# A perceiver kernel on one core: the second layers of the tiles ahead of the last are placed in fewer, denser pieces

## The chip, the cores and the metric

The kernel runs on one NeuronCore of a Trainium2 chip. The metric is the device time of one execution in microseconds (us). Before the change the median of three runs is 2055.67 us (2054.99 to 2056.97).

## What is computed

The input is 32 sequences of 64 rows and 256 columns, and for each sequence a context of 1601 rows of 256 columns. Two layers follow each other, each residual:

```python
x = x + L0_xattn(layernorm(x), ctx)    # a linear layer of x and of the mean of the context
x = x + L0_attn(layernorm(x))          # 16 heads, 64 keys
x = x + L0_ffn(layernorm(x))           # shared and routed experts
x = x + L1_xattn(layernorm(x), ctx)    # 16 heads over all 1601 context rows
x = x + L1_attn(layernorm(x))          # causal convolution, minimal GRU, gated feed-forward
x = x + L1_ffn(layernorm(x))           # two quantised linear layers with a gelu between
```

The last two lines are what the kernel calls the second layer of a tile. In L1_attn each part is normalised by its root mean square, then: a depthwise convolution of 4 taps and a 256x256 linear layer; gates per head and a first-order recurrence over 64 rows; silu(n w_gate) * (n w_value) w_out with 682 inner columns. L1_ffn rounds its activations to 8 bits by the row's largest absolute value, multiplies by ternary weights (256x1024), applies gelu, rounds again and multiplies by ternary weights (1024x256).

## The kernel before, in words

The 2048 rows are 16 tiles of 128 rows (two sequences each), taken in the order of `order`; `pos` counts them from 0 to 15. Nearly all time goes to L1_xattn. Its context is cut into pieces: 13 for each tile (`NU`), so the main loop runs over 208 pieces, `for g in range(NU * NT)`. One pass is called a slot here. Slots 195 to 207 belong to the last tile.

The order of the instructions on TensorE, VectorE, ScalarE and GpSimd is written out by hand (`tc.manual_schedule`), and each engine works its instructions in that order. TensorE's order in a slot g is:

1. `column_scores(g)`: scores `s` (L845, L851); ScalarE then makes two exponentials `pt` (L857) out of them, into a pair of PSUM buffers `sc` that scores and row scores share.
2. `maxima_rows`, in every third slot, and `values(g + 4)`: `vps` (L236), copied to `vau` by VectorE (L787).
3. place 0: steps of the other layers.
4. `row_scores(g + 5)`: `r` (L803), whose maxima `mx` VectorE takes (L810); in every third slot five short instructions follow (`maxima`).
5. place 0.5, then `weighted(g)`: `o` (L875), which needs both `pt` and collects the output.
6. `keys(g + 6)`: `kps` (L248), copied to `kt` by ScalarE (L770).
7. place 1: steps of the other layers. Here `in_columns` is set, and `mmq` splits a matmul into four of 32 columns, as the keys are.

The last slots have less: `values` end with slot 203, row scores with slot 202 and keys with slot 201.

All other layers are generators, cut into steps by `yield`. An object of the class `Steps` (L1245) runs a generator's steps over a stretch of slots: `planned(gen, t0, t1, n, place)` (L1337) spreads n steps evenly from t0 to t1 (in sixteenths of a tile). With place 3, at most one step runs at a place, and the value that the last `yield` gave says at which one: `ACT` at place 0, `COL` at place 0.5, anything else at place 1. What is left after the last slot runs in turns, one step of each generator at a time, in the loop `while plan` at the end of the function, together with the second layer of the last tile; this stretch is called the drain here.

The second layer of a tile (`recurrent`, then `bit_ffn`) has 30 steps. Those with TensorE work are marked PE:

```
 1 moments e (L192-L197)           11 PE tp_f, nT            21 PE ff (second half), th, m
 2 xn_e, yb                        12 PE hg, tanh gg zz, rr  22 m
 3 square, rn_e                    13 zz, gg, gg             23 PE ffo, x5, moments h
 4 xs_e                            14 gg, cc, scan           24 xn_h, am_h, qt, q_h
 5 PE tp_e, ypad                   15 PE gru, y2, xy         25 PE tpq_h, qT_h
 6 convolution, first half         16 square, rn_g           26 PE h1, gelu (L1124)
 7 convolution, second half        17 xs_g                   27 am_i, qs_i, qd_i
 8 PE pw, y1                       18 PE tp_g, nT2           28 L1070, L1071, q_i (L1074)
 9 square, rn_f                    19 PE ff (first half), th, m   29 PE tpq_i, qT_i
10 xs_f                            20 m                      30 PE h2, x6, store
```

Their pace is set in one line of the plan, L1348 (33 steps over 29.5 sixteenths, some 24 slots):

```python
planned(second_layer(pos - 1), 16 * pos + 1.5, 16 * pos + 31, 33, 3)
```

Counted out, this gives for the last three tiles that run in the loop: tile 12 (by position) from slot 171 to slot 191; tile 13 from slot 184 to slot 204; tile 14 from slot 197 on, with steps 1 to 15 in the loop (8 in slot 202, 11 in slot 204, 12 in 205, 15 in 207) and steps 16 to 30 in the drain, in turns with the 30 steps of tile 15.

Of the kernel before, what the change touches and what calls it, by code (L numbers as in the profile page):

```python
# [15 lines left out]
P = 128  # L16
# [28 lines left out]
def perceiver_kernel(ctx: ExitStack, tc: tile.TileContext, a: dict, out: bass.AP):  # L45
# [16 lines left out]
    ACT = "ACT"  # L62

    COL = "COL"

    def sc_tile(name):
        return ps_sc.tile([P, 2, 512], F32, tag="sc", name=name)
# [137 lines left out]
    def rms_scaled(x, name):  # L205

        xs = work_tile([P, D], "xs", f"xs_{name}")
        ss = small.tile([P, 1], F32, tag="ss", name=f"ss_{name}", bufs=4)
        nc.scalar.activation(xs, x, AF.Square, accum_out=ss)
        rn = small.tile([P, 1], F32, tag="rn", name=f"rn_{name}", bufs=4)  # L210
        nc.gpsimd.tensor_scalar(rn, ss, 1e-24, None, ALU.max)
        nc.gpsimd.tensor_tensor(rn, rn, mhalf, ALU.pow)
        yield
        nc.vector.tensor_scalar(xs, x, rn, None, ALU.mult)
        return xs

# [37 lines left out]
    def silu_mul(m, u, v, th):  # L254

        nc.scalar.activation(th, u, AF.Tanh, scale=0.5)
        nc.vector.tensor_scalar(m, u, 0.5, None, ALU.mult)
        nc.vector.tensor_tensor(m, m, v, ALU.mult)
        yield
        nc.vector.scalar_tensor_tensor(m, th, 1.0, m, ALU.add, ALU.mult)  # L260


# [689 lines left out]
    def recurrent(ti, x):  # L952
        def tile_(shape, tag, name):
            return work_tile(shape, tag, f"{name}_{ti}")

        m = moments(x, f"e{ti}")
        yield
        y = normalised(tile_([P, D], "xnb", "xn_e"), m)
        yb = plus_row(tile_([P, D], "xbb", "yb"), y, R_PWB)
        yield ACT  # L960
        xs = yield from rms_scaled(y, f"e{ti}")
        yield ACT
        t = transposed_ps(xs, f"e{ti}")
        cT = tile_([P, 2, 2, S], "xs", "cT")
        for c in range(2):
            nc.scalar.activation(ypad[:, c, :, 3:], t[:, c, :].rearrange("p (b s) -> p b s", b=2), AF.Copy,
                                 scale=gains[:, c, 0:1])
        yield
        for c in range(2):
            nc.vector.tensor_scalar(cT[:, c], ypad[:, c, :, 3:], chv[:, c, DW + 3:DW + 4], chv[:, c, DWB:DWB + 1],  # L970
                                    ALU.mult, ALU.add)
            for j in range(3):
                nc.vector.scalar_tensor_tensor(cT[:, c], ypad[:, c, :, j:j + S], chv[:, c, DW + j:DW + j + 1],
                                               cT[:, c], ALU.mult, ALU.add)
            yield
        o = mm_tile([P, D], f"pw_{ti}")
        mmq2(o, lambda c: cT[:, c].rearrange("p b s -> p (b s)"), lambda c: w_pw[:, c, :])
        y = tile_([P, D], "xnewb", "y1")
        nc.vector.tensor_tensor(y, o, yb, ALU.add)  # L979
        yield ACT  # L980
        xs = yield from rms_scaled(y, f"f{ti}")
        yield ACT

        t = transposed_ps(xs, f"f{ti}")
        nT = tile_([P, 2, P], "xTb", "nT")
        for c in range(2):
            nc.scalar.activation(nT[:, c, :], t[:, c, :], AF.Copy, scale=gains[:, c, 1:2])
        yield ACT

        def gt(name):  # L990
            return tile_([P, 2, 2, P], "g2k", name)

        gg, zz, rr = gt("gg"), gt("zz"), gt("rr")

        nc.gpsimd.memset(rr[DI:, :, :, :], 0.0)

        hg = [mm_tile([DI, 2, 2, P], f"hg_{ti}_{h}") for h in range(2)]
        for part in range(2):  # L1000
            for c in range(2):
                for h in range(2):
                    r = slice(64 * h, 64 * h + 64)
                    nc.tensor.matmul(hg[h][:, part, c, :], lhsT=w_hg[r, c, part * DI:(part + 1) * DI],  # L1004
                                     rhs=nT[r, c, :], start=True, stop=True)
        for h in range(2):
            nc.scalar.activation(gg[:DI, h], hg[h][:, 0], AF.Tanh, scale=0.5)
            nc.scalar.activation(zz[:DI, h], hg[h][:, 1], AF.Tanh, scale=0.5)
            nc.vector.tensor_scalar(rr[:DI, h], hg[h][:, 0], 0.0, 0.5, ALU.max, ALU.add)
        yield  # L1010
        hT = rr
        gg, zz, rr = (t[:DI] for t in (gg, zz, rr))
        nc.gpsimd.tensor_scalar(zz, zz, 0.5, 0.5, ALU.mult, ALU.add)
        nc.vector.tensor_scalar(gg, gg, 0.0, 0.5, ALU.min, ALU.mult)
        nc.vector.tensor_tensor(gg, gg, rr, ALU.add)
        yield
# [12 lines left out]
        nc.vector.tensor_tensor(y2, o, y, ALU.add)  # L1029
        xy = tile_([P, D], "xbb", "xy")  # L1030
        nc.gpsimd.tensor_tensor(xy, x, y2, ALU.add)
        yield ACT
# [7 lines left out]
        yield ACT  # L1040
        m = tile_([P, NF, P], "w4k", "fm")
        for f0 in range(0, NF, 3):
            uv = [mm_tile([P, 3, P], f"ff_{ti}_{f0}_{j}") for j in range(2)]
            for o, w in zip(uv, (w_fg, w_fv)):
                for f in range(3):
                    mm2(o[:, f, :], lambda c: w[:, c, (f0 + f) * P:(f0 + f + 1) * P], lambda c: nT[:, c, :])
            th = tile_([P, 3, P], "g2k", f"fth{f0}")
            yield from silu_mul(m[:, f0:f0 + 3, :], uv[0], uv[1], th)
            yield ACT if f0 == 0 else None
        o = mm_tile([P, D], f"ffo_{ti}")  # L1050
        for f in range(NF):
            mmq(o, m[:, f, :], w_fo[:, f, :], f == 0, f == NF - 1)
        x = tile_([P, D], "xnewb", "x5")
        nc.vector.tensor_tensor(x, o, xy, ALU.add)
        return x


    def quantised(v, n, tmp, sw, name):
# [7 lines left out]
        d = small.tile([P, 1], F32, tag="qd", name=f"qd_{name}", bufs=4)  # L1066
        nc.vector.tensor_tensor(d, am, sw, ALU.mult)
        if n == HID:
            yield
# [42 lines left out]

    def bit_ffn(ti, x):
        m = moments(x, f"h{ti}")
        yield
# [3 lines left out]
        yield ACT  # L1119
        h = work_tile([P, HID], "w4k", f"h_{ti}")  # L1120
        for j in range(2):
            h_ps = mm_tile([P, 512], f"h1_{ti}_{j}")
            mm2(h_ps, lambda c: qT[:, c, :], lambda c: w_b1[:, c, 512 * j:512 * j + 512])
            nc.scalar.activation(h[:, 512 * j:512 * j + 512], h_ps, AF.Gelu, scale=d)  # L1124
        yield
# [119 lines left out]
    class Steps:  # L1245
# [15 lines left out]

        def run(self, t, place):
            at = place if self.place == 2 and place != 0.5 else self.place
            if self.place == 3:
                if {ACT: 0, COL: 0.5}.get(self.kind, 1) != place:
                    return
                at = place
            if at == place:
                now = t + (0.5 * place if self.place >= 2 else 0)
                while self.gen is not None and self.done * (self.t1 - self.t0) <= (now - self.t0) * self.n:  # L1270
                    self.step()
                    if self.place == 3:
                        break

        def all(self):
            while self.gen is not None:
# [65 lines left out]
    for pos in range(1, NT):  # L1342
# [2 lines left out]
            planned(first_layer(pos), t0, t0 + 27 - 4 * (pos == 3), 28, 3)  # L1345
        if pos < NT - 1:
            planned(queried(pos), 16 * (pos - 1) + (1 if pos > 1 else 5), 16 * (pos - 1) + 8.5, 6, 0)
        planned(second_layer(pos - 1), 16 * pos + 1.5, 16 * pos + 31, 33, 3)  # L1348
    for group, t0, t1 in ((range(4, 6), 5.5, 15), (range(6, 9), 16, 42), (range(9, 13), 45, 84), (range(13, 16), 88, 140)):
        planned(sums_of(group), t0, t1, 12 * len(group) + 2, 0)  # L1350
    for c, t0 in ((1, 72), (2, 128), (3, 184)):
# [132 lines left out]
```

## Time and profile before

| what | value |
|---|---|
| median of three runs | 2055.67 us |
| profiled execution, own time | 2057.83 us |
| its span | 2056.1 us |
| TensorE (PE) busy | 1959.6 us, 95% |
| VectorE (DVE) busy | 1300.7 us, 63% |
| ScalarE (ACT) busy | 903.2 us, 44% |
| GpSimd (POOL) busy | 325.5 us, 16% |
| slots 203 to 207 | 1954.33 to 1983.14 us from the span's start |
| drain | 1983.14 to 2056.10 us |

The profiled execution is 2.16 us over the median of the other runs. A row of the timeline gives the start, the summed duration, the engine, the line, the operation, output<-input with shapes, the number of instructions, and in brackets the idle time before it with what ended it. Matmuls of fp32 count as two instructions each. Durations of one matmul overlap with those of its neighbours, so what a group of matmuls costs is best read from start to start.

### The profile page before, as it was taken

How to read it: one execution, taken by the hardware profiler on the slowest of the kernel's cores; microseconds unless marked ns; L12 is line 12 of the kernel's file. 1: busy time of each engine (PE TensorE's matmuls, PEld its weight loads, DVE VectorE, ACT ScalarE, POOL GpSimd, SP SyncE). 2: the span in 40 equal slices, each digit the busy share in tenths (PEclk: the TensorE clock that was granted, in tenths of full speed). 3: DMA queues.
4: the chain of work that ended last, by engine and by line, in shares of the span. 5: the costliest groups of instructions: out<-in, count | busy, mean ns of one | idle time of the engine just before them, and what ended most of it. 6: DMA issues, size and time to landing. Idle time of an engine off the chain costs nothing.

```text
span 2056.1 us, 79668 instructions
## 1 busy us (share of the span) xinstructions
PE 1959.6 (95%) x36755; PEld 1368.4 (67%) x36771; DVE 1300.7 (63%) x2618; ACT 903.2 (44%) x1402; POOL 325.5 (16%) x543
## 2 busy tenths in 40 slices
PE   5889999999999999999999999999999999999974
PEld 3556676667676766666766676767666666666663
DVE  4556766666657766666667666666667666565544
ACT  4345455454546444444544434343443434334431
POOL 2121111111112111111111121211110111000011
PEclk9899999999999999999999999999999999999986
DMA  9224323221222212112120101111011111101000
GB/s 310 105 87 171 128 85 111 77 88 44 94 89 88 95 44 72 46 58 76 61 77 20 58 22 37 50 40 45 26 59 32 61 44 37 57 3 48 2 12 5
DMA packets 54806, 136.90 MB, mean 67 GB/s; under 512 B 13318, under 2 KB 35016, under 8 KB 54472
## 3 DMA queue, kind: packets, MB, share of 16 engines
q1 hardware_dynamic: 53912, 130.99, 18.6%
q8 instruction: 288, 4.72, 0.9%
q10 hardware_dynamic: 560, 0.81, 0.1%
q14 instruction: 46, 0.38, 0.1%
HBM read 125.53 MB, written 6.25 MB: 64 GB/s over the span
## 4 chain that ended last, share of the span: by engine, by line
PE 86%; DVE 8%; ACT 2%; issue 2%; POOL 1%; DMA 0%; SPq 0%; DVEq 0%; POOLq 0%; ACTq 0%
PE vps L236 17%; PE kps L248 15%; PE r L803 11%; PE o L875 9%; PE s L851 9%; PE ff L236 4%; PE s L845 3%; DVE mx L810 3%; PE ffo L248 2%; PE q L236 1%; ACT pt L857 1%; PE wo L248 1%; PE hg L1004 1%; PE k L236 1%; PE sv L236 1%
## 5 line engine op out<-in xcount | busy, mean ns | idle before, releaser
L857 ACT ACTIVATE pt<-s 128x1024 f32<-128x1024 f32 (+1 forms) x416 | 403.1, 1021 | 267.6 <-PE s L851 267.5
L810 DVE TENSOR_REDUCE mx<-r 128x2 f32<-128x1024 f32 x384 | 451.9, 1219 | 98.3 <-PE r L803 97.9
L236 PE MATMUL vps<-w_L_xattn_WvT,ctxT 128*128 128x128 f32 x3072 | 391.6, 281 | 2.3 <-DVE y L979 1.8
L770 ACT ACTIVATE kt<-kps,chv 128x512 f32<-128x512 f32 x192 | 132.0, 687 | 586.1 <-PE kps L248 568.6
L236 PEld LDWEIGHTS vps<-w_L_xattn_WvT,ctxT 128*128 128x128 f32 x3072 | 357.9, 191 | 22.2 <-issue 3.7
L248 PE MATMUL kps<-ctxT,w_L_xattn_WkT 128*32 128x512 f32 x2992 | 356.1, 593 | 0.0
L787 DVE COPY vau<-vps 128x512 f32<-128x512 f32 (+1 forms) x208 | 143.6, 691 | 313.9 <-PE vps L236 312.5
L875 PEld LDWEIGHTS o<-pt,vau 128*32 128x32 f32 (+1 forms) x13312 | 198.8, 110 | 132.2 <-issue 118.5
L875 PE MATMUL o<-pt,vau 128*32 128x64 f32 (+1 forms) x13312 | 231.1, 221 | 5.2 <-ACT pt L857 5.1
L803 PE MATMUL r<-kt,qbd 32*128 32x512 f32 x1536 | 229.2, 647 | 2.8 <-DVE mx L810 2.0
L851 PE MATMUL s<-qbd,kt 32*128 32x128 f32 x6144 | 209.6, 272 | 0.0
L851 PEld LDWEIGHTS s<-qbd,kt 32*128 32x128 f32 x6144 | 207.2, 188 | 3.1
L248 PEld LDWEIGHTS kps<-ctxT,w_L_xattn_WkT 128*32 128x32 f32 x2992 | 83.5, 110 | 112.7 <-issue 112.7
L803 PEld LDWEIGHTS r<-kt,qbd 32*128 32x128 f32 x1536 | 66.3, 184 | 40.6 <-issue 19.8
L845 PEld LDWEIGHTS <-onesb 3*128 3x128 bf16 x768 | 21.3, 91 | 104.0 <-issue 102.1
L845 PE MATMUL s<-neg,onesb 3*128 3x512 bf16 x768 | 82.8, 386 | 5.8 <-DVE mx L810 5.0
L294 ACT ACTIVATE part<-part 128x1601 f32<-128x1601 f32 x48 | 74.1, 1544 | 0.0
L236 PE MATMUL ff<-nT,w_fg 128*128 128x128 f32 x384 | 51.0, 285 | 1.0 <-ACT nT L1039 1.0
L370 POOL TENSOR_TENSOR kbd<-kT,mask 128x512 f32<-128x512 f32 x32 | 32.6, 1041 | 114.8 <-ACT kT L363 114.8
L236 PEld LDWEIGHTS ff<-nT,w_fg 128*128 128x128 f32 x384 | 47.9, 201 | 1.8 <-ACT nT L1039 1.8
L236 PE MATMUL ff<-nT,w_fv 128*128 128x128 f32 x384 | 48.5, 276 | 0.0
L417 POOL TENSOR_TENSOR s<-s,mx 128x1024 f32<-128x1024 f32 x15 | 28.5, 1903 | 115.2 <-DVE mx L401 115.2
(384 smaller groups left out, 2397.8 us busy)
## 6 DMA issues: line engine op xcount, KB each, us to landing
ctxT<-ctxT SPq DMA_DIRECT2D x31, 1601.0 KB
part<-ctxT SPq DMA_DIRECT2D x60, 800.5 KB
od<-osb SPq DMA_DIRECT2D x15, 256.0 KB
rest<-ctxT SPq DMA_DIRECT2D x32, 65.0 KB
x<-x SPq DMA_DIRECT2D x16, 128.0 KB
out<-x SPq DMA_DIRECT2D x16, 128.0 KB
w<-w SPq DMA_DIRECT2D x16, 128.0 KB
rs<-od SPq DMA_DIRECT2D x30, 64.0 KB
```

Of the source, the lines that this page charges most:

```text
L236: nc.tensor.matmul(o, lhsT=lhsT(c), rhs=rhs(c), start=(c == 0), stop=(c == 1))
L248: nc.tensor.matmul(o[r], lhsT=lhsT[:, r], rhs=rhs, start=start, stop=stop)
L294: nc.scalar.activation(parts[j], parts[j], AF.Copy, accum_out=csum[:, c, 2 * i + b:2 * i + b + 1])
L370: nc.gpsimd.tensor_tensor(kbd[oc], kT[:, oc, :].rearrange("p (b k) -> p b k", b=2).unsqueeze(2).to_broadcast([P, 2, 4, S]), mask4.unsqueez ...
L770: nc.scalar.activation(kt, o, AF.Identity, bias=chv[:, hf.oc, BK2:BK2 + 1])
L787: nc.vector.tensor_copy(v[:kr, :, 0:VW - 16].rearrange("p k (h d) -> p k h d", d=17)[:, :, :, 0:16], o[:kr].rearrange("p k (h d) -> p k h ...
L803: nc.tensor.matmul(o, lhsT=qbd[r, q % 2, q // 2].rearrange("p h q -> p (h q)"), rhs=w.kt[r, q, :] if h is None else halves[h].kt[k][r, :], ...
L810: nc.vector.tensor_reduce(w.mx[:, 2 * m:2 * m + 2, h % 4, k], ps[m], AX.X, ALU.max)
L845: nc.tensor.matmul(o, lhsT=onesb[r, :], rhs=halves[h].neg[r, :].unsqueeze(1).to_broadcast([3, 4, P]), start=True, stop=False)
L851: nc.tensor.matmul(ps[i // 2][:kr, i % 2, j * P:(j + 1) * P], lhsT=w.kt[r, j, :] if h is None else halves[h].kt[k][r, j * P:(j + 1) * P], ...
L857: nc.scalar.activation(pt[:kr].rearrange("p i k c -> p i (k c)"), ps[m][:kr], AF.Exp)
L875: nc.tensor.matmul(w.o[32 * c:32 * c + 32, q, m, :], lhsT=v[:kr, j, 17 * hd:17 * hd + 32], rhs=pts[m][:kr, c // 2, j, c % 2 * S:c % 2 * S ...
```

## The change

Three things are changed.

First, the second layers' `yield`s say more: `OFF` and `OFF_ACT` mean that the next step has no TensorE work, `ANY` that it may run at place 0 or at place 1 (the two halves of ff, and h1; for these `mm2` becomes `mmq2`, so that at place 1 they are split into columns). Under place 3 the new values mean what the old ones did.

Second, there is a place 4 (`paced`). At a place that is due it runs either one step with TensorE work (`ACT` at place 0, `None` at place 1, `ANY` at both), and behind it at place 1 also the steps without TensorE work that are due; or, if the next step has no TensorE work, all such steps that are due, up to the next one that has.

Third, the plan's line sets: tile 12 ends two sixteenths earlier under place 3, tile 13 runs 33 steps over 18.5 sixteenths under place 4, and tile 14 runs 38 over 13.5, also under place 4.

```diff
+        def paced(self, t, place):
+            due = (t + 0.5 * place - self.t0) * self.n / (self.t1 - self.t0)
+            made = False
+            while self.gen is not None and place != 0.5 and self.done <= due:
+                off = self.kind in (OFF, OFF_ACT) or self.done == 0
+                if made and (place == 0 or not off):
+                    break
+                if not off:
+                    if made is not False or self.kind != ANY and (0 if self.kind == ACT else 1) != place:
+                        break
+                self.step()
+                made = made or not off or None
...
-        planned(second_layer(pos - 1), 16 * pos + 1.5, 16 * pos + 31, 33, 3)
+        t1, n, place = {NT - 3: (29, 33, 3), NT - 2: (20, 33, 4), NT - 1: (15, 38, 4)}.get(pos, (31, 33, 3))
+        planned(second_layer(pos - 1), 16 * pos + 1.5, 16 * pos + t1, n, place)
```

Counted out by hand from this code, the steps stand so (slot.place; the numbers are the steps of the list above):

```
tile 12 before: ... 184.0 19  184.1 20  185.0 21  185.1 22  186.1 23  187.1 24  188.0 25  189.0 26  189.1 27  190.1 28  191.0 29  191.1 30
tile 12 after:  the same slots and places
tile 13 before: 184.1 1   185.1 2   186.0 3   186.1 4   187.0 5   187.1 6   188.1 7   189.1 8   190.0 9   190.1 10  191.0 11  192.0 12
                192.1 13  193.1 14  194.1 15  195.0 16  195.1 17  196.0 18  197.0 19  197.1 20  198.0 21  198.1 22  199.1 23  200.1 24
                201.0 25  202.0 26  202.1 27  203.1 28  204.0 29  204.1 30
tile 13 after:  184.0 1,2  184.1 3  185.0 4  186.0 5  186.1 6,7  187.1 8,9,10  188.0 11  189.0 12  189.1 13,14  190.1 15,16  191.0 17
                192.0 18  192.1 19,20  193.0 21  193.1 22  194.1 23,24  195.0 25  195.1 26,27  196.0 28  197.0 29  197.1 30
tile 14 before: 197.1 1   198.1 2   199.0 3   199.1 4   200.0 5   200.1 6   201.1 7   202.1 8   203.0 9   203.1 10  204.0 11  205.0 12
                205.1 13  206.1 14  207.1 15, then 16 to 30 in the drain
tile 14 after:  197.0 1,2,3  197.1 4  198.0 5  198.1 6,7  199.1 8,9,10  200.0 11  201.0 12  201.1 13,14  202.1 15,16,17  203.0 18
                203.1 19,20  204.0 21  204.1 22  205.1 23,24  206.0 25  206.1 26,27,28  207.0 29  207.1 30
```

The drain then holds the second layer of tile 15 alone. The work itself, its instructions and their operands, is otherwise the same.

More of the change, by code (lines that the diff above doesn't have):

```diff
@@ L64, in perceiver_kernel @@
     COL = "COL"
+    ANY = "ANY"
+    OFF = "OFF"
+    OFF_ACT = "OFF_ACT"
     def sc_tile(name):
@@ L212, in rms_scaled @@
         nc.gpsimd.tensor_tensor(rn, rn, mhalf, ALU.pow)
-        yield
+        yield OFF
         nc.vector.tensor_scalar(xs, x, rn, None, ALU.mult)
@@ L258, in silu_mul @@
         nc.vector.tensor_tensor(m, m, v, ALU.mult)
-        yield
+        yield OFF
         nc.vector.scalar_tensor_tensor(m, th, 1.0, m, ALU.add, ALU.mult)
@@ L956, in recurrent @@
         m = moments(x, f"e{ti}")
-        yield
+        yield OFF
         y = normalised(tile_([P, D], "xnb", "xn_e"), m)
         yb = plus_row(tile_([P, D], "xbb", "yb"), y, R_PWB)
-        yield ACT
+        yield OFF_ACT
         xs = yield from rms_scaled(y, f"e{ti}")
@@ L967, in recurrent @@
                                  scale=gains[:, c, 0:1])
-        yield
+        yield OFF
         for c in range(2):
@@ L974, in recurrent @@
                                                cT[:, c], ALU.mult, ALU.add)
-            yield
+            yield OFF if c == 0 else None
         o = mm_tile([P, D], f"pw_{ti}")
@@ L979, in recurrent @@
         nc.vector.tensor_tensor(y, o, yb, ALU.add)
-        yield ACT
+        yield OFF_ACT
         xs = yield from rms_scaled(y, f"f{ti}")
@@ L1009, in recurrent @@
             nc.vector.tensor_scalar(rr[:DI, h], hg[h][:, 0], 0.0, 0.5, ALU.max, ALU.add)
-        yield
+        yield OFF
         hT = rr
@@ L1015, in recurrent @@
         nc.vector.tensor_tensor(gg, gg, rr, ALU.add)
-        yield
+        yield OFF
         nc.vector.tensor_tensor(gg, gg, zz, ALU.mult)
@@ L1031, in recurrent @@
         nc.gpsimd.tensor_tensor(xy, x, y2, ALU.add)
-        yield ACT
+        yield OFF_ACT
         xs = yield from rms_scaled(y2, f"g{ti}")
@@ L1039, in recurrent @@
             nc.scalar.activation(nT[:, c, :], t[:, c, :], AF.Copy, scale=gains[:, c, 2:3])
-        yield ACT
+        yield ANY
         m = tile_([P, NF, P], "w4k", "fm")
@@ L1045, in recurrent @@
                 for f in range(3):
-                    mm2(o[:, f, :], lambda c: w[:, c, (f0 + f) * P:(f0 + f + 1) * P], lambda c: nT[:, c, :])
+                    mmq2(o[:, f, :], lambda c: w[:, c, (f0 + f) * P:(f0 + f + 1) * P], lambda c: nT[:, c, :])
             th = tile_([P, 3, P], "g2k", f"fth{f0}")
             yield from silu_mul(m[:, f0:f0 + 3, :], uv[0], uv[1], th)
-            yield ACT if f0 == 0 else None
+            yield ANY if f0 == 0 else None
         o = mm_tile([P, D], f"ffo_{ti}")
@@ L1068, in quantised @@
         if n == HID:
-            yield
+            yield OFF
         nc.vector.tensor_scalar(tmp, v, s, 127.0, ALU.mult, ALU.min)
@@ L1114, in bit_ffn @@
         m = moments(x, f"h{ti}")
-        yield
+        yield OFF
         n = normalised(work_tile([P, D], "xnb", f"xn_h{ti}"), m)
@@ L1118, in bit_ffn @@
         qT, d = yield from quantised(n, D, tmp, sw1, f"h{ti}")
-        yield ACT
+        yield ANY
         h = work_tile([P, HID], "w4k", f"h_{ti}")
@@ L1122, in bit_ffn @@
             h_ps = mm_tile([P, 512], f"h1_{ti}_{j}")
-            mm2(h_ps, lambda c: qT[:, c, :], lambda c: w_b1[:, c, 512 * j:512 * j + 512])
+            mmq2(h_ps, lambda c: qT[:, c, :], lambda c: w_b1[:, c, 512 * j:512 * j + 512])
             nc.scalar.activation(h[:, 512 * j:512 * j + 512], h_ps, AF.Gelu, scale=d)
-        yield
+        yield OFF
         qT, d = yield from (halved(h, sw2, f"i{ti}") if ti == order[-1] else quantised(h, HID, h, sw2, f"i{ti}"))
@@ L1263, in run @@
             at = place if self.place == 2 and place != 0.5 else self.place
+            if self.place == 4:
+                self.paced(t, place)
+                return
             if self.place == 3:
-                if {ACT: 0, COL: 0.5}.get(self.kind, 1) != place:
+                if {ACT: 0, ANY: 0, OFF_ACT: 0, COL: 0.5}.get(self.kind, 1) != place:
                     return
```

## The prediction

> **What bounds the kernel now.** First the page: TensorE is busy for 95% of the span and carries 86% of the chain that ended last. Its clock row is full but for the last two slices.
>
> ```profile
> span 2056.1 us, 79668 instructions
> PE 1959.6 (95%) x36755; PEld 1368.4 (67%) x36771; DVE 1300.7 (63%) x2618; ACT 903.2 (44%) x1402; POOL 325.5 (16%) x543
> PEclk9899999999999999999999999999999999999986
> PE 86%; DVE 8%; ACT 2%; issue 2%; POOL 1%; DMA 0%; SPq 0%; DVEq 0%; POOLq 0%; ACTq 0%
> ```
>
> Then the busy times by stretch (length, then PE, PEld, DVE, ACT, POOL): slots from about 183 on, the next two, the last five, the drain.
>
> ```profile
> 1780.00:1940.00 160.00, 159.01 (x3036) 107.79 (x3036) 95.64 (x174) 61.09 (x91) 13.58 (x28) 1.00 0.09 32
> 1940.00:1954.33 14.33, 14.28 (x289) 9.63 (x288) 9.91 (x22) 8.17 (x10) 0.41 (x1) 1.00 0.01 2
> 1954.33:1983.14 28.81, 21.38 (x623) 17.65 (x620) 13.64 (x32) 13.98 (x20) 4.64 (x10) 0.87 0.07 21
> 1983.14:2056.10 72.96, 40.66 (x214) 30.96 (x212) 34.04 (x84) 13.83 (x33) 11.94 (x23) 0.66 0.01 4
> ```
>
> Up to slot 202 TensorE is full: what is added there costs its length. In the last five slots it idles 7.4 us, in the drain 32 us. TensorE's waits in 1780 to 1954 are one line, and those of the last five slots three:
>
> ```profile
> PE r L803 <- ACT pt L857: 0.9, 2, 0.5
> ...
> PE o L875 <- ACT pt L857: 5.1, 7, 1.2
> PE tpq_i L1079 <- POOL q_i L1074: 2.0, 1, 2.0
> PE s L845 <- DVE mx L810: 0.2, 1, 0.2
> ```
>
> So before slot 203 the old spacing leaves nearly no step waiting. Last the timeline of the drain: tile 15 (x, xs_e, rn_f, y) waits behind tile 14 (ff, q_h, q_i).
>
> ```profile
> 1987.35 0.42 DVE L948 TENSOR_TENSOR x<-wo,xb 128x256 f32<-128x256 f32 x1 [1.38 <-PE wo L244]
> 1994.84 0.35 DVE L214 TENSOR_SCALAR xs_e<-xn_e,rn_e 128x256 f32<-128x256 f32 x1
> 2007.41 0.23 POOL L211 TENSOR_SCALAR rn_f<-ss_f 128x1 f32<-128x1 f32 x1
> 2023.27 0.42 DVE L1029 TENSOR_TENSOR y<-gru,y 128x256 f32<-128x256 f32 x1 [1.11 <-PE gru L244]
> ```
>
> **1. The drain gets shorter: -12.7 us.** Steps 16 to 30 of tile 14 leave it. From x to the y after gru tile 15 now needs 2023.27 - 1987.35 = 35.9 us. Alone, with the rows' durations: x, st, mv, rstd, xn_e 2.6; square, rn_e (after yb's 0.73 on POOL), xs_e 2.1; tp_e 0.66, ypad, two convolutions of 1.5: 4.2; the second half of pw 1.2 and y 0.4; square, rn_f, xs_f 2.0; tp_f 0.65, nT, hg 2.0 up to rr 4.9 (hg starts 2011.17, rr ends 2014.87: 3.7); L1014, L1015, L1017, zz, scan 3.8; gru 1.8. With gaps that is 23.1 us, 12.8 less. The places where it is won show in the rows: xs_e waits 3.1 for the ff maxima of tile 14, rn_f 2.8 behind its q_h, gg and zz 2.5 behind its L1070 and q_i. After y nothing changes but a table load: tile 14's gelu brought the table that tile 15's used; alone, the load (1.28) starts at the end of qT_h (2042.91) and gelu at 2044.2, not 2044.04, so 0.2 back: 12.65. Ends 11 to 14: the clock, and GpSimd's zz, which took 1.05 here and 0.62 in slot 205.
>
> **2. Full slots get more TensorE work: +3.8 us.** Against slots 203 to 207 before, five steps move ahead of slot 203, and pw from 202 to 199. Start to start, fast clock: tpq_i 0.45, h2 0.98, tp_f 0.32, hg 1.05, pw 0.98. gru takes pw's old place in slot 202, where the scores wait for mx anyway. Sum 3.8; 3.4 if pw stays hidden in part, 4.6 by busy times (0.62, 1.06, 0.39, 1.12, 1.05, with 0.4 for waits). The halves of ff split into columns I price as unsplit (2.75 each): ffo, 48 split matmuls of twice the length, takes 2.71. The store of step 30 moves with it (tile 13 from 204 to 197, tile 14 from the drain to the end of 207); SP has nothing behind it that the end waits for: 0.
>
> **3. The last five slots: +7.8 us.** They now take 28.8 us from the scores of slot 203 to picked. After, counted from those scores: s, tpm and vps end at 3.85 and tp_g, waiting for xs_g, at 4.65; o 0.95, ff 2.7, s 1.3, ff 2.8, o 0.95, s 1.25: 14.6; two exponentials and the second part of o: 17.5; ffo 2.7: 20.2. Now chains with nothing to fill them. From ffo to q_h: in the drain x5 starts at 2037.21 and q_h ends at 2042.06, 4.9: 25.1, while TensorE has only s(206) of 1.2. tpq_h 0.4; o(206) 0.95; h1 1.2; second gelu 0.75: 28.4. am_i 1.22, four short ones 0.65, L1070 and L1071 1.44, q_i 1.05, gaps: 4.6, so tpq_i starts at 33.0; tpq_i 0.8, o(207) 1.2, h2 1.5: 36.6. Since picked is behind h2 in TensorE's order, all of tile 15 waits for this. 36.6 - 28.8 = +7.8. Ends: 6.5 with the fast clock throughout, 11.2 with half of it from ffo on.
>
> The clock in rows: equal scores in slots 205 and 206, the first after TensorE had waited 2.0 us for q_i.
>
> ```profile
> 1967.50 1.81 PE L851 MATMUL s<-qbd,kt 32*128 32x128 f32 x32
> ...
> 1972.56 1.06 PE L851 MATMUL s<-qbd,kt 32*128 32x128 f32 x32
> ```
>
> [...]
>
> **4. New waits in slots 184 to 202: +6.9 us.** The trace has none of these spacings; the bounds come from its rows.
> - ffo and q_h's chain in 194.1, tpq_h in 195.0: 4.9 us of chain behind s 1.2 and vps 1.9: TensorE waits 1.8, and with it all behind it.
> - h1 in 195.1: kt, then gelu to 2.5 us behind h1, the exponentials' table 1.28, the exponentials to 5.75. The row scores of 201 need their buffers and would write the second at 3.65: 2.1. (Place 0 costs 0.95: the two waits at 1851 and 1852, of tile 12, which stay.)
> - VectorE in front of mx and vau: rr behind gelu and tanh in 189, then am_i, gg, scan, some 7 us of VectorE in 189.1, where maxima also stand: 3.2; moments and xn_e in 184.0 (0.9), y and xs_f behind xn_h to qt in 187.1 (0.9), q_i beside normalise in 196 (0.6), 201.1 (0.35): 6.0 together. Buffers and the idle of VectorE (37% of the span) may hide part of it, so half: 3.0.
>
> Together 6.9. Ends: 0 if all is hidden, 9.9 in full. A gain is left out, as there is only 0.9 us of waiting to win.
>
> **Sum.** -12.7 + 3.8 + 7.8 + 6.9 = +5.8 us. The profiled execution took 2057.83 us (span 2056.1), so such a one would take 2063.6; it lies 2.2 over the median, so the forecast is 2055.67 + 5.8 = 2061.5 us. The terms' ends give -14 + 3.4 + 6.5 + 0 = -4.1 to -11 + 4.6 + 11.2 + 9.9 = +14.7.
>
> [...]
>
> **Rivals.** *Faster: the idle of the last five slots takes the work.* They have 7.4 us of idle TensorE. What comes in (tp_g 0.4, ff 5.5, ffo 2.7, tpq_h 0.4, h1 0.8, tpq_i 0.6, h2 1.0: 11.4) less what goes out (tpq_i 0.62, tp_f 0.39, h2 1.73, hg 1.12, gru 0.8: 4.7) is 6.7, less than that. If idle fits work, term 3 is 0, and with term 4 at 0 the change gives -12.7 + 3.4 = -9.3: 2046.4. For it: the 5.1 us of waits for pt are filled by ff. Against: the chains to q_h and q_i are 9.5 us with 1.2 us of scores in each, and picked stands behind them. It decides if these slots grow by less than 4.8 us with term 4 at 0. 0.12.
>
> *The same: nothing waits before slot 203.* Term 4 falls to between 0 and 5: VectorE and the buffers take the denser steps. -1.1 to +3.9: about 2057. For it: 0.9 us of waits now. Against: the two TensorE-side waits, 1.8 and 2.1, follow from the order alone. 0.28.
>
> *It doesn't do what it says*, the steps standing elsewhere: counted out, every place has at most one PE step of a tile, and tile 14 ends in 207.1. No chance of its own.
>
> **How the numbers follow.** This kernel's measurement tells about 0.2%, 4.1 us, from no change. The forecast case, slower by over that, has 0.60; its own range is 2060 to 2069. Within 0.2% 0.28, faster 0.12, mostly the first rival. The range leaves out the upper ends added up (0.08) and the first rival's (0.12): 2052 to 2069.
>
> **What would show it.** In the changed profile: drain from picked to the end near 60 us, not 73, with y about 23 us behind x; slots 203 to 207 near 36 us, and PE waits of 3 to 4 us each for q_h (tpq_h) and q_i (tpq_i); a PE wait of about 2 us for q_h near slot 195, and r waiting for pt in 196. Wrong would be: slots 203 to 207 at 30 us, or PE waits before them still near 1 us.

## The result, and the profile after

The changed kernel takes 2069.6 us (median of six, 2065.7 to 2072.9) against 2055.35 us for the kernel before (median of six beside it, 2054.95 to 2058.34). The ratio is 1.0065, 95% interval 1.0052 to 1.0079: slower, as forecast, and just above the upper end of the range (2069). The profiled execution took 2067.71 us, 9.9 us more than that of before.

The page of the changed kernel, the lines that answer to those of before:

```profile
span 2066.0 us, 80143 instructions
PE 1958.2 (95%) x36999; PEld 1365.3 (66%) x36999; DVE 1301.5 (63%) x2618; ACT 906.0 (44%) x1404; POOL 324.0 (16%) x543
PEclk9899999999999999999999999999999999999985
PE 85%; DVE 9%; ACT 3%; issue 2%; POOL 1%; DMA 1%; SPq 0%; DVEq 0%; ACTq 0%; POOLq 0%
```

No engine is busy for much longer: TensorE's busy time even falls by 1.4 us, and ScalarE's grows by 2.8, nearly all of it two more loads of a function table (1.28 us each). So the 10 us are waits, or work off TensorE's best clock, and the busy times by stretch say where. Each row is a stretch of the changed kernel: slots 184 to 202 (called the full slots here), slots 203 to the start of picked (TensorE's first matmuls of the drain), and from there to the end; then its length and the busy time of PE, PEld, DVE, ACT, POOL, the granted clock and DMA.

```profile
1794.83:1966.05 171.22, 163.38 (x3238) 113.23 (x3235) 104.29 (x197) 69.52 (x102) 16.35 (x32) 1.00 0.05 17
1966.05:2005.63 39.58, 29.07 (x764) 23.29 (x758) 15.47 (x40) 16.89 (x22) 5.13 (x12) 0.88 0.05 13
2005.63:2066.00 60.37, 26.78 (x132) 19.11 (x128) 23.81 (x58) 9.17 (x23) 7.74 (x16) 0.61 0.01 5
```

The first of these cuts in the profile of before (the other two, of 28.81 and 72.96 us, are the last rows of that view in the prediction):

```profile
1795.58:1954.33 158.75, 157.71 (x3062) 109.26 (x3062) 95.54 (x179) 64.79 (x92) 13.20 (x27) 1.00 0.05 17
```

The full slots are 12.5 us longer: 5.7 of busy TensorE and 6.8 of idle. The last five slots are 10.8 longer, the drain 12.6 shorter, and slot 184 starts 0.75 earlier. What TensorE waited for, in slots 184 to 202 (the first five lines) and in 203 to 207 (the last three), by the view of waits (total us, times, longest):

```profile
PE r L809 <- ACT pt L863: 2.5, 3, 1.7
PE tpq_h L1085 <- POOL q_h L1080: 1.8, 1, 1.8
PE s L851 <- DVE mx L816: 1.7, 3, 0.7
PE tp_f L226 <- DVE xs_f L220: 1.0, 1, 1.0
PE hg L1010 <- ACT h L1130: 0.9, 1, 0.9
...
PE tpq_i L1085 <- POOL q_i L1080: 3.8, 1, 3.8
PE tpq_h L1085 <- POOL q_h L1080: 3.7, 1, 3.7
PE o L881 <- ACT pt L863: 1.8, 2, 1.2
```

Both waits that were named ahead of the run in the full slots are there (q_h 1.8 us against 1.8, pt 1.7 against 2.1), and both in the last slots (3.7 and 3.8 against 3 to 4). Last the timeline of the drain, tile 15 alone, the rows that answer to the four of before:

```profile
2008.85 0.42 DVE L954 TENSOR_TENSOR x<-wo,xb 128x256 f32<-128x256 f32 x1 [0.79 <-PE wo L250]
2013.15 0.35 DVE L220 TENSOR_SCALAR xs_e<-xn_e,rn_e 128x256 f32<-128x256 f32 x1 [1.80 <-POOL rn_e L218]
2020.11 0.22 POOL L217 TENSOR_SCALAR rn_f<-ss_f 128x1 f32<-128x1 f32 x1 [6.99 <-ACT xs_f L215]
2032.64 0.42 DVE L1035 TENSOR_TENSOR y<-gru,y 128x256 f32<-128x256 f32 x1 [2.12 <-PE gru L250]
```

From x to y it is 23.8 us now (before 35.9), and each wait is for the step just ahead in tile 15's own chain, none for tile 14.

### The profile page after: what moved, and what is told of

The parts are those of the page before. It is cut to its first block, busy times and chain, and to the rows that moved or that the text cites. A ratio compares the mean times of both kernels' runs of the same rounds, so it can differ in the third digit from the quotient of the medians.

```text
span 2066.0 us, 80143 instructions
## 1 busy us (share of the span) xinstructions
PE 1958.2 (95%) x36999; PEld 1365.3 (66%) x36999; DVE 1301.5 (63%) x2618; ACT 906.0 (44%) x1404; POOL 324.0 (16%) x543
## 4 chain that ended last, share of the span: by engine, by line
PE 85%; DVE 9%; ACT 3%; issue 2%; POOL 1%; DMA 1%; SPq 0%; DVEq 0%; ACTq 0%; POOLq 0%
PE vps L242 17%; PE kps L254 15%; PE r L809 11%; PE o L881 9%; PE s L857 8%; PE ff L250 4%; PE s L851 3%; DVE mx L816 3%; PE ffo L254 2%; PE q L242 1%; ACT pt L863 1%; PE wo L254 1%; PE hg L1010 1%; PE k L242 1%; PE h L254 1%
## 5 line engine op out<-in xcount | busy, mean ns | idle before, releaser
L376 POOL TENSOR_TENSOR kbd<-kT,mask 128x512 f32<-128x512 f32 x32 | 32.6, 1041 | 114.8 <-ACT kT L369 114.8
L250 PE MATMUL ff<-nT,w_fg 128*128 128x128 f32 x360 | 46.6, 281 | 0.5 <-ACT nT L1045 0.5
L263 DVE TENSOR_SCALAR fm<-ff 128x384 f32<-128x384 f32 x32 | 17.8, 558 | 45.4 <-ACT fth L262 45.4
```

Source lines behind the costliest of these rows:

```text
L250: nc.tensor.matmul(o, lhsT=lhsT, rhs=rhs, start=start, stop=stop)
```

## The experiments

**The same kernel again, and each half alone.** Four kernels, run beside the kernel before (2056.77). The plan's entries by tile:

```diff
 e4: {NT - 3: (29, 33, 3), NT - 2: (20, 33, 4), NT - 1: (15, 38, 4)}   # the change
 e1: {NT - 3: (29, 33, 3), NT - 2: (20, 33, 4)}                        # tile 13 only
 e2: {NT - 1: (15, 38, 4)}                                             # tile 14 only
 e3: {NT - 1: (20, 33, 4)}                                             # tile 14 only, slower: steps 1 to 24 in the loop
```

> The changed kernel once more, for a second profiled execution: its executions range over 7 us where those of the kernel before range over 3.4. My theory: the stretches that differ are the last five slots and the waits before them, where TensorE idles and its clock falls at one execution and not at the other; up to slot 183 both profiles agree within 1 us, and the drain within 1.5. Rival C: the difference lies before slot 183, where the two kernels have the same instructions, so it would be no work of the change. Time 2066 to 2073 us by both.

Measured: 2067.83 us, ratio 1.0061 [1.0047, 1.0074]. The profile has 171.20, 38.14 and 60.71 us for the three stretches. The lengths of slots 184 to 202 repeat. As expected, the last five slots differ most, by 1.4: TensorE has half its clock there for 6.8 us, and for 9.2 in the first profile. The drain differs by 0.3, the start of slot 184 by 1.2, a little over the 1 that was expected.

> Only tile 13 gets the new pace (place 4, done in slot 197); tile 14 keeps the old one, with steps 16 to 30 in the drain. My theory: the full slots pay for it, work 1.4 (tpq_i and h2 ahead of slot 203) and waits about 7 (for q_h 1.8, for the exponentials in 196 1.7 and a slow clock behind it 0.9, for mx, xs_f and gelu the rest), the last five slots give back 2.4 to 3 (no tpq_i that waits for q_i), the drain is as before: +6 to +7, 2061 to 2063 us. Rival A (the loss is made in the last five slots alone, denser steps before them cost nothing): -2 to +1, 2053 to 2056 us.

Measured: 2064.18 us, 1.004 [1.0025, 1.0054], a little over what was expected. Full slots 171.32; last five 24.0; drain 73.6. TensorE's waits in the full slots are line for line those of the changed kernel, so these waits belong to tile 13. That the full slots are as long as with both tiles is a coincidence. Without tile 14's steps slots 198 to 202 are 1.5 us shorter than in the change; but slot 195 takes 11.5 us and not 9.9, since TensorE had half its clock there (the last section shows it). The last five slots are 4.8 us under the profile of before, but both stretches hold some half clock. Slots 203 and 204, which have none in e1 and in e9 below, take 9.0 us against 12.1, so 3.1 is what tile 13's steps give back there.

> Only tile 14 gets the new pace (place 4, done in slot 207); tile 13 keeps the old one, done in slot 204. My theory: full slots +2.4 of work and 0.8 of waits, last five slots +10.8 as in the changed kernel and up to 1.4 more for tile 13's tpq_i and h2, drain -12.6: +1.5 to +3, 2057 to 2058.5 us. Rival A: nearly the whole loss of the changed kernel is here, +10 to +13, 2065 to 2068 us.

Measured: 2065.41 us, 1.0044 [1.0028, 1.0059], more than expected. Full slots +3.3 and drain -13.8 are near what was expected; the last five slots took 45.2 us, not about 40. In slot 203 both tiles now meet on VectorE. The timeline of TensorE, then of VectorE:

```profile
1965.08 0.47 PE L226 MATMUL tp_g<-ident,xs_g 128*128 128x128 f32 x2 [2.39 <-DVE neg L834]
```

```profile
1960.30 1.21 DVE L1067 TENSOR_REDUCE am_i<-h 128x1 f32<-128x1024 f32 x1
...
1962.07 0.42 DVE L1035 TENSOR_TENSOR y<-gru,y 128x256 f32<-128x256 f32 x1
1964.35 0.58 DVE L220 TENSOR_SCALAR xs_g<-y,rn_g 128x256 f32<-128x256 f32 x1 [1.86 <-POOL rn_g L218]
1964.85 0.20 DVE L834 COPY neg<-tpm 128x128 bf16<-128x128 bf16 x1
1964.98 0.67 DVE L793 COPY vau<-vps 128x512 f32<-128x512 f32 x1
```

Tile 13's am_i to qd_i stand ahead of tile 14's y, so xs_g is late, and neg and vau behind it: VectorE idles for 1.86 us ahead of xs_g and starts neg only at 1964.85, though tpm, from which neg is copied, ended at 1960.85. That tile 13 is out of the way by then is what its denser pace buys: 5.6 us in the last slots (45.2 against 39.6), for 9.1 in the full ones (162.1 against 171.2). Part of the 5.6 is the clock, since e2's last five slots hold 13.7 us at half clock and the change's 9.2.

> As the run with tile 14 alone, but its pace is slower (33 steps over 18.5 sixteenths), so that its steps 1 to 24 stand in the loop (ff in 205 and 206, ffo in 207) and 25 to 30 in the drain: the two chains to q_h and q_i no longer stand between the last scores and picked. My theory: full slots +2.4, last five slots +2 to +3 (ff fills the waits for the exponentials), drain -6 to -9, since the ff and xs_e waits of tile 15 are gone and those for the rounding are left: -5 to 0, 2050 to 2055 us. Rival B (whatever is left of tile 14 in the drain delays tile 15 as much as all of it does): drain 0, so +4 to +5, 2060 us.

Measured: 2065.35 us, 1.0045 [1.0032, 1.0057], where 2050 to 2055 was expected; the last five slots are 34.8 us, 6.0 longer and not 2 to 3, and the drain is 71.1 us, 1.8 shorter and not 6 to 9. What is left of tile 14 starts behind picked and runs in turns with tile 15. Timeline of TensorE:

```profile
1993.40 0.65 PE L250 MATMUL wo<-w_o,oT 128*128 128x256 f32 x2
1997.64 1.22 PE L250 MATMUL wo<-w_o,oT 128*128 128x256 f32 x2 [3.59 <-DVE oT L938]
...
2007.82 1.03 PE L1085 MATMUL tpq_i<-identb,q_i 128*128 128x128 bf16 x8 [6.38 <-POOL q_i L1080]
2008.65 0.64 PE L226 MATMUL tp_e<-ident,xs_e 128*128 128x128 f32 x2
```

VectorE does tile 14's x to qt before oT of tile 15, which is late by 3.6 us; then tp_e stands in TensorE's order behind tpq_i of tile 14 and 6.4 us of wait. So what shortens the drain is not how many steps leave it, but that no step of tile 14 stands ahead of one of tile 15.

**The last five slots without tile 14's rounded layers, and tile 13 with more room.** The kernel before took 2055.78 beside them.

```diff
 e5:  def tail(...):           # after the recurrent part of the tile at position 14
+         if ti == order[NT - 2]:
+             nc.sync.dma_start(out[ti * P:(ti + 1) * P, :], x)
+             return
 e6:  e1's plan, and in bit_ffn, for position 13 alone
-    yield OFF        # before xn_h to q_h
+    yield None if ti == order[NT - 3] else OFF
-    yield ANY        # before h1
+    yield ACT if ti == order[NT - 3] else ANY
```

> The changed kernel with steps 24 to 30 of tile 14 (its quantised layers) left out: x5 of that tile is stored in their place. Nothing else moves. My theory: the last five slots are long because the chains to q_h and q_i stand in TensorE's order before picked; without them ffo ends 21.2 after the scores of 203 and two slots of 4.3 follow, so 30 and not 39.6, drain unchanged at 60: -9 to -10 against the changed kernel, 2058 to 2060 us. Rival D (the slow clock of thin slots makes them long, the chain is beside it): 35 to 37, so -3 to -5, 2063 to 2066 us.

Measured: the last five slots take 30.1 us, as expected, with no half clock in them. So 9.5 of their 39.6 us come with tile 14's steps 24 to 30: the two chains to q_h and q_i, and the half clock behind their waits, which e12 below puts at 2.8 of the 9.5. The time, 2064.66 us, 1.0041 [1.0026, 1.0057], misses the 2058 to 2060; it fell by 3 to 5 us only (against e4 and the first median). In the profile slot 184 starts at 1800.7 instead of 1794.8, in front of anything that the edit touches, with 41.0 us at half clock ahead of it and not 27.3. Whether that holds for the other executions is not shown.

> Tile 13 alone with the new pace, as in the first run, but its step 24 stands one slot behind step 23 (195.1), and h1 (step 26) only at place 0 (197.0): no chain stands between ffo and tpq_h, and gelu's table load is no longer between h1 behind the keys and the next exponentials. Same work. My theory: the waits for q_h (1.8) and for the exponentials (1.7, and 0.9 to 2.5 of slow clock behind the two) go, 0.95 for a table load at place 0 comes: slots 184 to 202 shrink from 171.3 to 167 to 168, -3 to -4 against the first run, 2060 to 2061 us. Rival E (the denser work itself costs, the waits only show it): unchanged, 2063 to 2065 us.

Measured: 2062.85 us, 1.0035 [1.0023, 1.0048]. The full slots are 166.3 us, 5.0 shorter than in e1; 1.6 of this is e1's half clock in slot 195, which leaves 3.4 for the spacing. The times show little of it: 3 to 4 us were expected against e1, but the two ratios, 1.0035 and 1.004, have intervals that overlap. With q_h's chain one place earlier and h1 moved out of 195.1, the 1.8-us wait for q_h is gone, the largest one of r for pt is 0.5, and one of 0.9 for q_i has come (rows of e6's waits):

```profile
PE tpq_i L1085 <- POOL q_i L1080: 0.9, 1, 0.9
...
PE r L809 <- ACT pt L863: 0.8, 2, 0.5
```

**The drain from the other side.** Three kernels on the code of before. e7 gives tile 14 a step only in every second turn; e8 turns the order round, tile 15 first; e9 holds tile 14's steps 24 to 30 until tile 15 has done 18 steps.

```diff
 in the drain's loop `for s in list(plan)`, ahead of s.step():
 e7: +    if s is not last and last.gen is not None and turn % 2: continue
 e8: the loop itself: for s in reversed(list(plan))
 e9: +    if s is not last and s.done >= 23 and last.gen is not None and last.done < 18: continue
     and h of tile 14 in a buffer of its own
```

> The kernel before, loop unchanged; in the drain tile 14 takes a step at every second turn only, tile 15 at every turn. The drain's saving is looked for without moving work into the loop. My theory: tile 15 waits for tile 14 since a step of tile 14 stands one turn behind its forerunner and each engine keeps its order; two turns apart it is ready, and only its busy time is left: drain -4 to -8, 2048 to 2052 us. Rival F (it is the shared busy time, and rounding now meets rounding): 0 to +4, 2055 to 2060 us.

> The kernel before, loop unchanged; in each turn of the drain the step of tile 15 stands ahead of that of tile 14. My theory: xs_e no longer stands behind the ff maxima of tile 14, nor rn_f behind its q_h: -1 to -4, 2052 to 2055 us. Rival F: 0.

Measured: e7 2060.64 us, 1.0022 [1.001, 1.0034], drain 72.8 as before; e8 2060.2 us, 1.0027 [1.0017, 1.0037], drain 78.8. Both miss. In e8 x to y even takes 41.2 us: GpSimd's rstd_h of tile 14 stands ahead of tile 15's rn_f, as tile 14's steps did before. In e7 y after gru does come 29.1 us behind x, not 35.9, but tile 14's later steps are put off so far that they now stand ahead of what follows that y. The timeline of GpSimd, where rn_g is tile 15's, and of TensorE:

```profile
2017.78 0.23 POOL L196 TENSOR_SCALAR rstd_h<-mv_h 128x1 f32<-128x1 f32 x1 [3.75 <-DVE mv_h L194]
2018.09 0.57 POOL L197 TENSOR_TENSOR rstd_h<-rstd_h,mhalf 128x1 f32<-128x1 f32 x1
2018.74 0.22 POOL L211 TENSOR_SCALAR rn_g<-ss_g 128x1 f32<-128x1 f32 x1
```

```profile
2020.15 0.41 PE L220 MATMUL tp_g<-ident,xs_g 128*128 128x128 f32 x2 [3.60 <-DVE xs_g L214]
```

GpSimd does rstd_h of tile 14 first, and that waits for tile 14's x behind ffo. The delay is not gone, only met later: turns hold the later chain wherever the other's long steps fall. The profile is the fastest of e7's twelve executions (2055.33 us), so where the 5 us of its median come from is not shown.

> The kernel before, loop unchanged; in the drain tile 14 takes its steps up to 23 (ffo) in turns as before, then waits until tile 15 has done 18 steps, so that its quantised layers (24 to 30) stand beside tile 15's ff, which keeps TensorE busy and leaves VectorE and GpSimd idle. Its h takes another buffer. My theory: of the 12.7 us that tile 15 loses to tile 14, 6 to 7 come from steps 24 to 30 (rn_f behind q_h, gg and zz behind L1070 and q_i); beside ff they cost some 3: drain 73 to about 69, so -3 to -4, 2051 to 2053 us. Rival F (only the sum of the work counts, wherever it stands): 0.

Measured: 2052.37 us against 2055.43 (12 runs and 23), ratio 0.9991 [0.9981, 1.0001]. In the profile the drain falls by 6.1 us, to 66.9, and x to y takes 28.1. The full slots keep their 158.75 us; the last five, whose code is unchanged, take 25.5 and not 28.8, with no half clock in them.

```profile
1982.65 0.42 DVE L948 TENSOR_TENSOR x<-wo,xb 128x256 f32<-128x256 f32 x1 [0.86 <-PE wo L244]
...
2010.71 0.42 DVE L1029 TENSOR_TENSOR y<-gru,y 128x256 f32<-128x256 f32 x1 [2.12 <-PE gru L244]
```

It is the only kernel of the study whose median is under that of before, by 3.1 us as expected, though the interval reaches 1. In the profile about half of the 12.7 us is had in the drain's own order, with no slot before it touched. That profile is the fastest of twelve, and its drain holds 32.6 us at half clock against 49.1 in that of before, so part of the 6.1 is the clock.

**Both ideas together, and the change with tile 13 spaced.** Run beside e9. e10: `{NT - 1: (22, 33, 4)}` with e9's hold. e11: the change with e6's two yields.

> Tile 14 alone with place 4, 33 steps over 20.5 sixteenths: steps 1 to 23 in the loop (ff in 205.1 and 206.1, ffo in 207.1), and 24 to 30 held back in the drain until tile 15 has done 18 steps. My theory: full slots +1.5 to +3, last five slots +4 to +5 (ff fills the waits for the exponentials, ffo stands before picked), drain -9 to -10.5, since tile 15 runs nearly alone: -1 to -4, 2051 to 2054 us. Rival F: the drain stays at 71, as with steps 25 to 30 in turns, so +6, 2061 us.

> The changed kernel with tile 13's step 24 one slot later and its h1 at place 0 only, as in the spaced run with tile 13 alone. My theory (the parts add up): -4 to -5 against the changed kernel, all of it in slots 195 to 198, 2063 to 2065 us. Rival E: unchanged, 2068 us.

Measured: e10 2057.8 us, 1.0012 [1.0003, 1.0021], above the 2051 to 2054 expected; drain -9.4 as expected, full slots +2.5, but the last five slots +9.0 where 4 to 5 were expected: TensorE is busy there for 8.8 us more, with 10.2 us at half clock against 7.3 in the profile of before. What the rest consists of is not shown. e11 2065.14 us, 1.005 [1.0037, 1.0063]; full slots 168.6, 2.6 shorter than the change's. That is 0.8 less than the 3.4 which the same edit gave without tile 14, and the 0.8 lies in slot 198, where the wait for q_i is now 1.2 and not 0.9. Against e6, tile 14's denser steps cost 2.3 us in the full slots.

**The clock by itself.** The changed kernel with work that nothing needs in the two waits of slots 206 and 207; the kernel before beside it took 2055.03.

```diff
 column_scores(g), behind the scores:
+        if g >= NU * NT - 2:
+            fill = mm_tile([P, 512], f"fill_{g}")
+            for c in range(13):
+                nc.tensor.matmul(fill, lhsT=identb, rhs=w_b1[:, 0, 0:512], start=(c == 0), stop=(c == 12))
```

> The changed kernel with 13 more matmuls of 128x512 bf16 behind the scores of slots 206 and of 207, whose result nothing reads; h1's four of this shape took 1.03, so 13 take some 3.2 us, less than the waits of 3.74 and 3.79 us for q_h and q_i that they fill. Theory (in those slots TensorE runs at a lower clock because it had idled): o of 206, h1, the scores of 207, o of 207 and h2 take 1.0, 1.0, 1.2, 1.0 and 1.0 from start to start, not 1.31, 1.89, 1.26 (with the row behind it), 1.71 and 1.87; slots 203 to picked take 37.0 us, not 39.6, close to the 36.6 plus 1.1 of the prediction with its left out terms; the drain is at most 0.5 shorter; the time is 2 to 3 us under that of the change, at 1.004 of before. Rival (these matmuls are long for another reason, such as where their operands lie or the exponentials' buffers): they keep their lengths and the slots take 39.6 or more, with the time at 1.0055 or above. Nothing else in the chains to q_h and q_i changes by either.

Measured: 2067.07 us, 1.0057 [1.004, 1.0073]. The 2 to 3 us that were expected did not come in the time, which the rival's 1.0055 or above fits. The lengths decide against the rival. The timeline of TensorE, first in the changed kernel, then with the filler:

```profile
1992.29 0.28 PE L1085 MATMUL tpq_h<-identb,q_h 128*128 128x128 bf16 x2 [3.74 <-POOL q_h L1080]
1992.50 1.55 PE L881 MATMUL o<-pt,vau 128*32 128x64 f32 x64
1993.81 1.95 PE L254 MATMUL h<-wq_L_ffn_w1T,qT_h 128*32 128x512 bf16 x16
...
2002.05 1.94 PE L881 MATMUL o<-pt,vau 128*32 128x64 f32 x64
2003.76 1.93 PE L254 MATMUL h<-wq_L_ffn_w2T,qT_i 128*32 128x256 bf16 x32
```

```profile
1985.20 3.80 PE L254 MATMUL ffo<-w_fo,fm 128*32 128x256 f32 x48
...
1993.95 0.29 PE L1089 MATMUL tpq_h<-identb,q_h 128*128 128x128 bf16 x2 [0.82 <-POOL q_h L1084]
1994.16 1.10 PE L885 MATMUL o<-pt,vau 128*32 128x64 f32 x64
1995.08 1.05 PE L254 MATMUL h<-wq_L_ffn_w1T,qT_h 128*32 128x512 bf16 x16
...
2002.37 1.10 PE L885 MATMUL o<-pt,vau 128*32 128x64 f32 x64
2003.55 1.06 PE L254 MATMUL h<-wq_L_ffn_w2T,qT_i 128*32 128x256 bf16 x32
```

With the waits filled, the four groups behind them have their short lengths, and from tpq_h to picked it takes 10.6 us instead of 13.3: idling is what made them long. Slots 206 and 207 take 7.1 and 8.5 us here, and 8.1 to 8.7 and 9.1 to 10.0 in the three profiles with the same instructions but no filler (the change, e4, e11). But slots 203 to picked take 38.2, not 37.0: this time ffo runs slow (3.7 us from start to start, against 2.7), behind the same waits of 1.2 and 0.6 us for pt that left it fast in the changed kernel; and slot 185, long before the edit, takes 12.7 us and not 11.0, with half clock. So the mechanism is shown, and its price in one execution depends on where it strikes.

## Why the prediction was right in sign and too small in size

**Term 1, the drain, -12.7: measured -12.6.** Right, and nearly so by its steps: x to y took 23.8 us against 23.1, so 12.1 of the 12.6 were won there. That the sum agrees to 0.1 is luck: picked to x took 1.0 less than before (3.2 against 4.2), which the forecast did not have, and y to the end 0.5 more, where it had put 0.2. The load of gelu's table stands alone at 2052.75 with 1.28 us, so the small loss put down for it is there, too. e3, e7 and e8 show the mechanism from outside: steps of tile 14 left in turns with tile 15 hold it; in e9 and e10, where the later ones wait, they hold it less.

**Terms 2 and 4, the full slots, 3.8 + 6.9 = +10.7: measured +12.5.** TensorE's idle time grew by 6.8, so the new waits were priced rightly in sum, though the halving of VectorE's part was a guess. Piece by piece: q_h in 195 1.8 against 1.8; r of 201, in slot 196, for pt 1.7 against 2.1; the waits for maxima (1.7), xs_f (1.0) and gelu (0.9), all in slots 185 to 190 behind VectorE or ScalarE, 3.6 against the halved 3.0. e1 shows that they all belong to tile 13, and e6 that the first two come from its spacing: 5.0 us less by two steps moved, 1.6 of it the half clock in e1's slot 195. Busy time grew by 5.7 against 3.8. Of the difference 0.9 is really a wait: the row scores of slot 196 are shown with 2.0 us, those one slot earlier with 1.1. It is not the slow clock that the expectations of e1 and e6 name: the granted clock is 1.00 there, and the second half of these scores starts 0.9 after the first, when the second of the two exponentials ends. With it the wait for pt is 2.6 against 2.1.

**Term 3, the last five slots, +7.8: measured +10.8.** This is the term that was too small, 3.0 of the 4.1 us that the profile is over the sum. By the prediction's own time table, counted from the scores of slot 203: ffo was to end at 20.2 and ends at 21.2; tpq_h was to start at 25.1 and starts at 26.2; tpq_i at 33.0 and 35.0; picked at 36.6 (its last terms add up to 36.5) and 39.6. So 1.0 is lost before the chains begin: tp_g itself (0.34) was left out of the sum and starts 0.2 late, the rest lies in scores and ff. The chains were right, 5.0 us to q_h against 4.9, and 4.6 to q_i against 4.6. The other 1.9 is in the groups behind the two waits, o, h1, o and h2 above all, which were summed near the fast clock (0.95, 1.2, 1.2 and 1.5). e12 shows that it is the clock: with the waits filled they need 0.9, 1.0, 1.2 and 1.0 from start to start, and not 1.3, 1.9, 1.7 and 1.9. The text had this as the upper end, 11.2 with half the clock from ffo on, and chose a value near the lower one (6.5) although it had itself put 3 to 4 us of waiting ahead of those groups. With 10.8 there the sum would have been +8.8.

The clock alone does not explain the 3.0, for the two sides were counted at different clocks. The 28.8 us of before hold 7.3 us at half clock; without any, in e7 and e9, the same slots take 25.5. The 36.6 was summed near the fast clock. Added up from profiles in which each slot has no half clock (8.9, 5.2, 6.9, 7.1 and 8.5 us), the changed slots take 36.5, an estimate; so at the fast clock on both sides the term is about +11.0, and with slow stretches on both sides +10.8. The mis-sized step is the subtraction 36.6 - 28.8: a nearly fast stretch less a partly slow one. That the 36.6 meets 36.5 is luck, too: 1.1 us of work was left out of it, and about 1 us of slow clock was in it.

In slots 206 and 207 the waits are 3.74 and 3.79 us, and half clock follows both, from 1992.98 and from 1999.81 us.

**The rest.** The medians lie 14 us apart (11 in e4's repetition), the profiles 10. The forecast took the 2.2 us by which the profile of before lies over its median as an offset of both kernels; the profile of the changed kernel lies 1.9 under its own. So of the 8.1 us between 2061.5 and 2069.6, 4.1 are in the terms and 4.0 in this offset. The code of the last five slots of before is unchanged in e7, e8 and e9, and takes 25.5, 28.9 and 25.5 us there; the profile of before, which the forecast was counted from, had 28.8. With 25.5 the three stretches would give 12.5 + 14.1 - 12.6 = 14.0. That most runs of before are of the shorter kind is argued from this, not shown.

**The rivals.** "Faster" fails at its point of decision: the last slots grew by 10.8, not under 4.8. The waits for pt did fall from 5.1 to 1.8 us, as it says, but the two for q_h and q_i came to 7.5, where only 2.0 for q_i had been. "The same" fails with waits of 6.8 us before slot 203. The signs named for the forecast came, but for the length of the last five slots (39.6, not near 36).

## What to carry to other kernels

Work moved out of a tail into full slots cost its length here (5.7 us more of busy TensorE in slots 184 to 202), and chains of short steps placed without room between them cost their waits as well (6.8 us there); with the last five slots 23 us went in to take 12.6 out, by the profiles. Before moving it, look at what the tail really waits for: two chains worked in turns held each other here (x to y of tile 15 took 35.9 us in turns with tile 14 and 23.8 alone), and holding the one with slack (e9) gave about half of the drain's gain in its profile and 3 us in the median, at no cost elsewhere. And a sum that sets a new stretch against an old one should take both at the same clock: look at the granted clock of the old one first, and where the new one has a wait as long as those for q_h and q_i (3.74 and 3.79 us), price the matmuls behind it at both clocks.

## What the runs showed of the hardware that was not expected

The lower clock came after much shorter idling than in slots 206 and 207, and not each time. The same wait, 1.75 us for q_h in slot 195, was followed by slow row scores and outputs in e1, and by fast ones in the changed kernel, e4 and e12, with the same instructions around it. Timelines of TensorE, e1 and then the change:

```profile
1904.32 0.28 PE L1085 MATMUL tpq_h<-identb,q_h 128*128 128x128 bf16 x2 [1.75 <-POOL q_h L1080]
1904.54 1.88 PE L809 MATMUL r<-kt,qbd 32*128 32x512 f32 x8
1906.34 1.94 PE L881 MATMUL o<-pt,vau 128*32 128x64 f32 x64
```

```profile
1905.33 0.28 PE L1085 MATMUL tpq_h<-identb,q_h 128*128 128x128 bf16 x2 [1.76 <-POOL q_h L1080]
1905.55 1.14 PE L809 MATMUL r<-kt,qbd 32*128 32x512 f32 x8
1906.62 1.10 PE L881 MATMUL o<-pt,vau 128*32 128x64 f32 x64
```

The busy times in narrow stretches, again e1 and then the change (length, PE, and the granted clock ahead of the last two columns), show what differs:

```profile
1901.41:1904.82 3.41, 1.66 (x17) 1.36 (x19) 2.59 (x9) 1.39 (x3) 0.50 (x2) 1.00 0.16 47
1904.82:1908.23 3.41, 3.41 (x76) 1.92 (x76) 1.80 (x2) 0.20 (x1) 0.00 (x0) 0.50 0.03 7
```

```profile
1900.82:1904.23 3.41, 2.76 (x44) 2.44 (x40) 2.20 (x10) 1.94 (x2) 0.80 (x2) 1.00 0.24 71
1904.23:1907.65 3.42, 2.32 (x78) 1.46 (x82) 1.97 (x4) 0.37 (x1) 0.41 (x1) 1.00 0.05 13
```

In the profiles of before and of the changed kernel every stretch at half clock lasts 3.41 us or a multiple of it, up to 30.72 us (but for the last, of 17.38 and 17.00 us, which the end of the profile cuts), and all its edges in one execution lie on one grid of 3.41 us. Where the grid lies differs between executions: an edge at 1965.65 us in before and one at 1983.84 us in e12 are 18.19 us apart, 5.3 cells of the grid. In e1 the whole wait falls into one cell of the grid, and the next cell has half clock. In the changed kernel the grid parts the same wait between two cells, and neither is followed by half clock. The two waits for pt in slot 205 went the same way: in e12 both fall into one cell (1980.43 to 1983.84, TensorE busy for 1.63 us) and ffo behind it is slow, in the changed kernel they are parted (busy for 2.33 and 2.72) and ffo is fast. How little work in a cell is enough is not settled: cells busy for 1.94 us (before, from 1962.24) and 2.21 us (e12, from 1802.95) were followed by half clock, one of 1.95 us (e12, from 1901.93) and one of 1.52 us (e7, from 2015.03) were not.

Beside this, the start of slot 184 lay between 1790.9 and 1800.7 us in the profiles, with the same instructions ahead of it. It goes with the time at half clock ahead of it: 17.1 us in the earliest (e8), 41.0 in the latest (e5). So single profiles of this kernel can be compared by stretches whose granted clock agrees, and only medians by their ends.
